# Splitting the contraction of narrow fp32 products into two row tiles, ordered through SyncE

## The chip, the core and the metric

The kernel runs on one core of a Trainium2 chip. The metric is the device time of one execution in microseconds. Two runs of the kernel before took 1523.30 and 1524.68 us, a median of 1523.99 us.

## What is computed

The reference, cut to what matters (B = 8, N = 4096, F = 256):

```python
HW = einsum('bnf,fo->bno', x, W)
A_norm = relu((adj + adj.T) * 0.5)
D = sum(A_norm, axis=1)
d = where(D > 0, D ** -0.5, 0)
L_norm = eye(N) - d[:, None] * A_norm * d[None, :]
out = relu(einsum('nm,bmo->bno', L_norm, HW))
return layernorm(x + out, axis=-1)
```

`adj` is sparse, and denser towards its first rows and columns.

## The kernel before

The first half of the kernel (to about 590 us) symmetrises `adj` in 512x512 blocks and writes it to the DRAM array `a_dram`, forms the scaled products `g = d * x W` (2048 columns: 8 batches of 256) and writes them to `g_dram`, and multiplies the first block of 128 output rows ("lead").

The last stage, which the change touches, computes the other 31 blocks of 128 output rows. They are taken in units `u` of two blocks, 2u+1 and 2u+2 (the last unit has one), in the order `SEQ`. Every row j of `g` gets a pattern of four bits for a unit: which of the four 64 row halves of the unit's two blocks have a nonzero among the 64 entries that meet it. Rows of one pattern ("kind") are listed, 128 to a list. For each list, `gather` (L797) issues two indirect DMAs on GpSimd: `ga` (L814), the 128 rows of `a_dram` that serve as the weights, and `g` (L827), the 128 rows of 2048 columns that stream through. A ring of 12 `g` tiles lets the gathers run ahead of the products.

`steps_of(u)` orders a unit's lists into steps. A step of kind 0, 3 or 12 has products of all 128 output rows of a block ("full"). A step of kinds 1+2, 4+8, 6, 9 or 5+10 has products of 64 output rows; most such steps have two that use different halves of TensorE's columns, some have four (two blocks), a few have one. At L1032 the products of a step are issued for c = 0 to 3, the four PSUM banks of 512 columns of each block:

```python
for c in range(G // S):
    for (b, rows, at, gt), new_rows in zip(work, fresh):
        ...
            nc.tensor.matmul(
                py[2 * u + 1 + b][c][rows, :],
                lhsT=at[:, off + rows.start : off + rows.stop],
                rhs=gt[:, c * S : (c + 1) * S],
```

What else belongs to a unit stands in the program's order around the products, written out by hand: `queue(engine)` ties an instruction behind the last one traced on that engine, and `after(n, fn)` defers work until n products later.

- When a block's last product is issued, `finish` lets ScalarE evict its four banks (`evict`, L683). A little later VectorE adds the residual (L693), takes the statistics (L702 and after) and an inverse root, and, three products later in program order, normalises (L726). Right behind it stands the store of the block on SyncE's queue, `nc.sync.dma_start(out...)` (L734).
- The first block of a unit ends in its steps of kinds 5+10 or before; the second ends with the unit's last step, 4+8 or 4.
- After the first block, TensorE runs the small products of the list building for later units (`lists`: L226 to L356), which VectorE reads and works on (`place`, `place_rest`, `index`). At the start of a unit `prepare` puts more list work on VectorE (`spread`, L335 to L351; `patterns`, L199 to L216).

In this stage SyncE does nothing but the 31 stores of whole blocks, and the four of the last block.

Of the kernel before, what the change touches and what calls it, by code (L numbers as in the profile page):

```python
# [59 lines left out]
def kernel(  # L60
# [25 lines left out]
    nc = tc.nc  # L86
    B, N, F = x.shape
    FO = w.shape[1]
    P = 128
    S = 512  # L90
# [4 lines left out]
    G = B * FO  # L95
# [2 lines left out]
    QU = 4  # L98
    HOLD = 10
    RING = 12  # L100
    EPS = 1e-5
    NK = len(KINDS)
    tiles = [sum(caps) for caps in CAPS]
# [71 lines left out]
    def blocks(u):  # L175

        return min(2, NB - 1 - 2 * u)
# [497 lines left out]
    def residual(i, engine):  # L675
        xr = blocks_pool.tile([P, B, F], F32, tag="adj", name=f"xr_{i}")
        engine.dma_start(xr, x[:, i * P : (i + 1) * P, :].rearrange("b p f -> p b f"))
        return xr
# [12 lines left out]
    def moments(i, y, z, stat):  # L691

        nc.vector.tensor_add(z, z, y)  # L693
        return statistics(i, z, stat)

    def statistics(i, z, stat, tag=""):
# [6 lines left out]
        for b in range(n):  # L703
            nc.vector.bn_aggr(mv[:, b, :], stats[:, b, :])
        nc.vector.tensor_scalar(rstd, mv[:, :, 1], EPS, None, ALU.add)
        return mv, rstd
# [32 lines left out]
    def targets(u, kind):  # L739

        if kind == 0:
            kind = 15 if blocks(u) == 2 else 3
        out = []
        for b in range(2):
            h = kind >> 2 * b & 3
            if h:
                out.append((b, {1: slice(0, Q), 2: slice(Q, P), 3: slice(0, P)}[h]))
        return out
# [19 lines left out]
    with (  # L768
        tc.tile_pool(name="ypool", bufs=2) as ypool,
        tc.tile_pool(name="rows", bufs=RING + 2) as apool,  # L770
        ExitStack() as gath,
    ):
        ring = [
            gath.enter_context(tc.tile_pool(name=f"gath_{k}", bufs=1)).tile([P, G], F32, name=f"g{k}")
            for k in range(RING)
        ]
# [9 lines left out]
            "pe": mybir.EngineType.PE,  # L786
            "act": mybir.EngineType.Activation,
            "dve": mybir.EngineType.DVE,
            "pool": mybir.EngineType.Pool,
        }  # L790

        def queue(engine):

            traced = reversed(nc.cur_bb.bb.instructions)
            return tc.issue_after(next(i for i in traced if i.engine == engines[engine]))

        def gather(n):  # L797

            if n >= len(order):
                return  # L800
            u, kind, t = order[n]
            both = len(targets(u, kind)) == 2
            at = apool.tile([P, 2 * P], F32, tag="a", name=f"ga_{u}_{t % tmax}")
            if t < 0:
                if not hub_loads:
                    with queue("pool"):
                        hub_loads.append(nc.gpsimd.dma_start(hub, g_dram[:P, :]))
                with queue("pool"):
                    nc.gpsimd.dma_start(at, a_dram[:P, (2 * u + 1) * P : (2 * u + 3) * P])
                got[u, t] = (at, hub)  # L810
                return
            gi, ai = plan[u]
            with queue("pool"):
                nc.gpsimd.indirect_dma_start(  # L814
                    out=at if both else at[:, :P],
                    out_offset=None,
                    in_=a_pairs if both else a_rows,
                    in_offset=bass.IndirectOffsetOnAxis(ap=ai[:, t : t + 1], axis=0),
                    element_offset=P if both else 0,
                )  # L820


            n = len(ring_tiles)
            gt = ring[n % RING]
            ring_tiles.append(gt)
            with queue("pool"):
                nc.gpsimd.indirect_dma_start(  # L827
                    out=gt,
                    out_offset=None,
                    in_=g_dram,  # L830
                    in_offset=bass.IndirectOffsetOnAxis(ap=gi[:, t : t + 1], axis=0),
                    bounds_check=N if n < RING else N - 1,
                    oob_is_err=False,
                )
            got[u, t] = (at, gt)
# [4 lines left out]
        def after(n, fn, *args):  # L840
            later.append((n, fn, args))
# [8 lines left out]
        u = SEQ[0]  # L850
        xr = {i: residual(i, nc.sync) for i in (0, *range(2 * u + 1, 2 * u + 1 + blocks(u)))}
        for n in range(RING):
            gather(n)
        n = RING
        py = {0: lead}
        left = {}
# [50 lines left out]
        def finish(i):  # L907

            if i == NB - 1:
                finish_last(i)  # L910
                return
            with queue("act"):
                y = evict(i, py.pop(i), ypool)

            def rest():
                z = xr.pop(i)
                with queue("dve"):
                    mv, var = moments(i, y, z, stat)
                with queue("dve"):
                    rstd = inverse_root(i, var, stat)  # L920

                def end():
                    in_turn(normalise, i, z, mv, rstd)

                after(3, end)

            after(1, rest)
# [59 lines left out]
        def in_turn(fn, *args):  # L987

            with queue("dve"):
                fn(*args)  # L990

        finish(0)
        side = None
        for q, (u, step) in enumerate(steps):
            new = q == 0 or steps[q - 1][0] != u
            last = q + 1 == len(steps) or steps[q + 1][0] != u
            if new:
                after(6, prepare, u)
                if q > 0:
                    after(10 if u != SEQ[-1] else 4, residuals, range(2 * u + 1, 2 * u + 1 + blocks(u)))  # L1000
                left = {}
                for v, st in steps[q:]:
                    if v == u:
                        for k, t in st:
                            for b, _ in targets(u, k):
                                left[b] = left.get(b, 0) + 1
                begun = set()
                for b in range(blocks(u)):
                    py[2 * u + 1 + b] = []
            work = [(b, rows, *got[u, t]) for m in range(2) for k, t in step for b, rows in targets(u, k)[m : m + 1]]  # L1010
            if work[0][1] == side != slice(0, P):
                work.reverse()
            side = work[-1][1]
            for b in sorted({wk[0] for wk in work}):
                if not py[2 * u + 1 + b]:
                    py[2 * u + 1 + b] = [
                        psum.tile([P, S], F32, tag=f"b{b}", name=f"py_{u}_{b}_{c}") for c in range(G // S)
                    ]
            fresh = []
            for b, rows, at, gt in work:  # L1020
                hs = {(b, h) for h in range(2) if rows.start <= h * Q < rows.stop}
                assert not hs & begun or hs <= begun
                fresh.append(not hs & begun)
                begun |= hs
                left[b] -= 1
            for c in range(G // S):
                for (b, rows, at, gt), new_rows in zip(work, fresh):
                    both = any(len(targets(u, k)) == 2 for k, t in step)
                    off = b * P if both else 0

                    with queue("pe"):
                        nc.tensor.matmul(  # L1032
                            py[2 * u + 1 + b][c][rows, :],
                            lhsT=at[:, off + rows.start : off + rows.stop],
                            rhs=gt[:, c * S : (c + 1) * S],
                            start=new_rows,
                            stop=left[b] == 0,
                            skip_group_check=True,
                        )
            for k, t in step:  # L1040
                gather(n)
                n += 1
            run_later(sum(1 + (rows == slice(0, P)) for _, rows, _, _ in work))
            for b in {wk[0] for wk in work}:
                if left[b] == 0:
                    finish(2 * u + 1 + b)
                    if b == 0:
                        after(2, lists, u)
# [9 lines left out]
    with tc.If(short > 0):  # L1058
        with (
# [4 lines left out]
            for i in range(NB):  # L1064
# [4 lines left out]
                py = [psum.tile([P, S], F32, tag="b0", name=f"pz_{i}_{c}") for c in range(G // S)]  # L1069
                for m in range(NB):  # L1070
                    gt = full.tile([P, G], F32, tag="g", name=f"gf_{i}_{m}", bufs=4)
                    nc.sync.dma_start(gt, g_dram[m * P : (m + 1) * P, :])
                    for c in range(G // S):
                        nc.tensor.matmul(
                            py[c],
                            lhsT=lt[:, m, :],
                            rhs=gt[:, c * S : (c + 1) * S],
                            start=(m == 0),
                            stop=(m == NB - 1),
# [33 lines left out]
```

## Time and profile before

| what | value |
| --- | --- |
| median of 2 runs | 1523.99 us |
| profiled execution, its span | 1527.5 us |
| last stage, first to last product of L1032 | 594.9 to 1513.8 us |
| mean granted TensorE clock | 0.981 |
| DMA, mean over the span | 370 GB/s |
| gathers of `g` (L827) / of `ga` (L814) on GpSimd | 268, mean 1101 ns / 268, mean 1090 ns |
| evictions (L683) | 120, mean 687 ns |
| residual adds (L693) | 31, mean 2294 ns |
| normalisations (L726) | 248 (eight per block), mean 409 ns |

How to read it: the profile is of one execution, and its span is the time from the first to the last instruction; the page's shares are of that span. A group's line has the line of the kernel, engine, operation, what is written and read, how often, busy time and mean length of one, and the idle time of the engine ahead of it with what ended it. Lengths of matmuls overlap, so a group's busy time is less than count times length. "128*64" is a matmul of 128 contracting rows and 64 columns of weights. Page slices and windows show the granted clock as PEclk.

### The profile page before, as it was taken

The page shows a single profiled execution, that of the slowest core. Times are in us where ns is not written, and L with a number is a line of the kernel's source. Part 1 is how long each engine was busy: PE and PEld are TensorE (multiplying, and loading weights), DVE is VectorE, ACT ScalarE, POOL GpSimd, SP SyncE. Part 2 cuts the span into 40 slices and gives each one's busy share as a digit, 9 for nine tenths or more (in the row PEclk, how much of TensorE's full clock was granted, in tenths as well). Part 3 has the DMA queues.
Part 4 walks back from the last instruction along what each step waited for, and adds up shares of the span by engine and source line. Part 5 has one row for each costly group of instructions (what it writes and reads, how often), then busy time and mean ns, then how long its engine had stood idle before and what let it go on. Part 6 is the DMA issues. An engine that isn't in the chain of part 4 may idle for free.

```text
span 1527.5 us, 19332 instructions
## 1 busy us (share of the span) xinstructions
PE 1441.2 (94%) x6440; PEld 763.6 (50%) x6440; DVE 983.6 (64%) x3015; ACT 369.0 (24%) x462; POOL 682.0 (45%) x1051
## 2 busy tenths in 40 slices
PE   5999999989989989999999999999999999999995
PEld 5778777767767754433343343333433433333331
DVE  4676578888646463055568769569137688898534
ACT  3655554535434450010100100100010010001111
POOL 3002010010303316666667666666556676656653
PEclk9999999989999999999999999999999999999998
DMA  9999999999879898999999999999979999999995
GB/s 340 365 366 401 393 379 365 359 369 354 344 248 367 332 390 354 401 395 418 361 393 372 402 409 365 393 403 389 384 278 406 346 394 403 405 393 366 379 405 195
DMA packets 216714, 564.50 MB, mean 370 GB/s; under 512 B 16550, under 2 KB 104918, under 8 KB 180134
## 3 DMA queue, kind: packets, MB, share of 16 engines
q0 software_dynamic: 54224, 304.94, 50.4%
q1 hardware_dynamic: 93472, 126.89, 23.8%
q10 hardware_dynamic: 68912, 131.37, 22.7%
q8 instruction: 54, 0.88, 0.2%
q14 instruction: 52, 0.43, 0.1%
HBM read 443.61 MB, written 136.34 MB: 380 GB/s over the span
## 4 chain that ended last, share of the span: by engine, by line
PE 68%; DMA 14%; DVE 9%; issue 5%; POOL 2%; ACT 2%; ACTq 0%; DVEq 0%; POOLq 0%
PE py L1032 49%; PE pg L532 8%; DMA g<-g_dram,gi 6%; PE lead L490 5%; DMA a_dram<-sym 5%; DVE sym L427 3%; PE xtr L521 2%; PE tr L423 2%; DVE part L432 2%; DMA xin<-in_x_dram 2%; DMA ga<-a_dram,ai 1%; ACT sym L431 1%; PE lists L356 1%; ACT xt L522 1%; POOL g L827 0%
## 5 line engine op out<-in xcount | busy, mean ns | idle before, releaser
L1032 PE MATMUL py<-g,ga 128*64 128x512 f32 (+1 forms) x2872 | 813.0, 600 | 18.4 <-DMA g<-g_dram,gi 8.0
L1032 PEld LDWEIGHTS py<-g,ga 128*64 128x64 f32 (+1 forms) x2872 | 293.1, 151 | 525.1 <-issue 493.1
L827 POOL DMA_INDIRECT g<-g_dram,gi x268 | 294.9, 1101 | 219.1 <-PE py L1032 79.1
L814 POOL DMA_INDIRECT ga<-a_dram,ai x268 | 292.0, 1090 | 109.5 <-issue 76.8
L683 ACT ACTIVATE y<-py,minus_r 128x512 f32<-128x512 f32 x120 | 79.9, 687 | 812.3 <-PE py L1032 659.8
L693 DVE TENSOR_TENSOR xr<-xr,y 128x2048 f32<-128x2048 f32 x31 | 71.1, 2294 | 269.1 <-ACT y L683 267.2
L532 PE MATMUL pg<-w_sb,xt 128*128 128x256 f32 x1024 | 232.0, 385 | 5.2 <-ACT xt L522 5.2
L427 DVE TENSOR_TENSOR sym<-tr,adj 128x512 f32<-128x512 f32 x256 | 162.7, 683 | 96.9 <-PE tr L423 80.2
L532 PEld LDWEIGHTS pg<-w_sb,xt 128*128 128x128 f32 x1024 | 195.6, 194 | 33.4 <-ACT xt L522 5.6
L432 DVE TENSOR_REDUCE part<-sym 128x32 f32<-128x2048 f32 x64 | 145.5, 2279 | 62.0 <-ACT sym L431 62.0
L423 PE MATMUL tr<-ident,adj 128*128 128x128 f32 x1024 | 138.4, 285 | 30.6 <-DVE sym L427 19.2
L431 ACT ACTIVATE sym<-sym 128x2048 f32<-128x2048 f32 x64 | 122.6, 1916 | 129.9 <-DVE sym L427 117.5
L452 POOL TENSOR_TENSOR r<-e,neg_half 128x4 f32<-128x4 f32 x8 | 8.3, 1039 | 317.9 <-DVE e L451 236.5
L423 PEld LDWEIGHTS tr<-ident,adj 128*128 128x128 f32 x1024 | 118.6, 146 | 60.4 <-DVE sym L427 32.1
L521 PE MATMUL xtr<-ident,xin 128*128 128x128 f32 x512 | 72.4, 288 | 18.0 <-DVE sym L427 16.5
L702 DVE BATCH_NORM_STATS2 stats<-xr 128x6 f32<-128x256 f32 x256 | 87.0, 413 | 1.1
L726 DVE TENSOR_SCALAR xr<-xr,mv,root 128x256 f32<-128x256 f32 x248 | 83.6, 409 | 0.1
L490 PE MATMUL lead<-gt,strip 128*128 128x512 f32 x176 | 83.0, 598 | 0.0
L522 ACT COPY xt<-xtr 128x512 f32<-128x512 f32 x128 | 68.1, 591 | 46.7 <-PE xtr L521 46.0
L542 ACT ACTIVATE gt<-pg,r 128x512 f32<-128x512 f32 x88 | 60.6, 688 | 74.8 <-PE pg L532 72.3
L1032 PE MATMUL py<-g_hub,ga 128*128 128x512 f32 x176 | 77.3, 592 | 0.0
L521 PEld LDWEIGHTS xtr<-ident,xin 128*128 128x128 f32 x512 | 59.0, 146 | 34.9 <-DVE sym L427 26.4
(142 smaller groups left out, 825.8 us busy)
## 6 DMA issues: line engine op xcount, KB each, us to landing
adj<-in_adj_dram SPq DMA_DIRECT2D x64, 1024.0 KB
a_dram<-sym ACTq DMA_DIRECT2D x64, 1024.0 KB
out_dram<-xr SPq DMA_DIRECT2D x31, 1024.0 KB
xr<-in_x_dram ACTq DMA_DIRECT2D x29, 1024.0 KB
xin<-in_x_dram SPq DMA_DIRECT2D x44, 512.0 KB
g_dram<-gt ACTq DMA_DIRECT2D x22, 1024.0 KB
xin<-in_x_dram POOLq DMA_DIRECT2D x20, 512.0 KB
g_dram<-held ACTq DMA_DIRECT2D x10, 1024.0 KB
```

The costliest lines, as they stand in the source:

```text
L423: ins = nc.tensor.transpose(pt[:, c * P : (c + 1) * P], tji[:, c, a * P : (a + 1) * P], ident)
L427: nc.vector.tensor_add(sym[:, a, :], pt, tij[:, a, :])
L431: nc.scalar.activation(sym, sym, AF.Relu, scale=0.5)
L432: nc.vector.tensor_reduce(part[:, i * A : (i + 1) * A, j * S // Q : (j + 1) * S // Q], sym.rearrange("p a (c q) -> p a c q", q=Q), AX.X, A ...
L490: nc.tensor.matmul(lead[c], lhsT=strip, rhs=g[:, c * S : (c + 1) * S], start=not done, stop=len(done) == NB - 1, skip_group_check=True,)
L521: nc.tensor.transpose(pt[:, k, c, :], xin[b // H][:, b % H + k, c * P : (c + 1) * P], ident)
L532: ins = nc.tensor.matmul(pg[:, k * FO : (k + 1) * FO], lhsT=xt[:, b + k, c, :], rhs=w_sb[:, c, :], start=(c == 0), stop=(c == FC - 1),)
L702: nc.vector.bn_stats(stats[:, b, :], z[:, b, :])
L726: nc.vector.tensor_scalar(z[:, b, :], z[:, b, :], mv[:, b, 0:1], rstd[:, b : b + 1], ALU.subtract, ALU.mult,)
L814: nc.gpsimd.indirect_dma_start(out=at if both else at[:, :P], out_offset=None, in_=a_pairs if both else a_rows, in_offset=bass.IndirectOff ...
L827: nc.gpsimd.indirect_dma_start(out=gt, out_offset=None, in_=g_dram, in_offset=bass.IndirectOffsetOnAxis(ap=gi[:, t : t + 1], axis=0), boun ...
L1032: nc.tensor.matmul(py[2 * u + 1 + b][c][rows, :], lhsT=at[:, off + rows.start : off + rows.stop], rhs=gt[:, c * S : (c + 1) * S], start=ne ...
```

## The change

A step whose products are all of 64 columns is split along the contracting rows (`KP = 2`): row tile 0 takes the partitions 0 to 63 of `ga` and `g`, row tile 1 the partitions 64 to 127. In group c, row tile 0 works on bank c and row tile 1 on bank (c + 2) % 4, so the two never write one bank in the same group. Full steps are as before.

From group c to c + 2 a bank passes from one row tile to the other. This order is kept through SyncE: after each group an empty instruction on SyncE (a "tick") waits for the group's last product, and the first product of the group after the next waits for that tick. The ticks are queued behind what was last traced on SyncE. In the program as built the tick is an event on SyncE's sequencer.

```diff
+    KP = 2
...
-            "pool": mybir.EngineType.Pool,
+            "pool": mybir.EngineType.Pool, "sp": mybir.EngineType.SP,
...
+        ticks = []
+
+        def follow(after_, before_):
+            tc.add_manual_dep(
+                after_.ins, before_.ins.name,
+                mybir.DependencyInfo(mybir.DependencyClass.Sync, mybir.DependencyReason.DATA),
+                reason="one bank, two row tiles",
+            )
...
+            few = all(rows.stop - rows.start < P for _, rows, _, _ in work)
+            nk = KP if few else 1
             for c in range(G // S):
-                for (b, rows, at, gt), new_rows in zip(work, fresh):
...
+                first_of_step = True
+                for kp in range(nk):
+                    cc = (c + kp * (G // S) // nk) % (G // S)
+                    ps = slice(kp * P // nk, (kp + 1) * P // nk)
+                    for (b, rows, at, gt), new_rows in zip(work, fresh):
...
+                            ins = nc.tensor.matmul(
+                                py[2 * u + 1 + b][cc][rows, :],
+                                lhsT=at[ps, off + rows.start : off + rows.stop],
+                                rhs=gt[ps, cc * S : (cc + 1) * S],
+                                start=new_rows and c < (G // S) // nk,
+                                stop=left[b] == 0 and c >= (nk - 1) * (G // S) // nk,
+                                skip_group_check=True,
+                            )
+                        if nk > 1:
+                            if first_of_step and len(ticks) > 1:
+                                follow(ins, ticks[-2])
+                            first_of_step = False
+                if nk > 1:
+                    with queue("sp"):
+                        ticks.append(nc.sync.nop())
+                    follow(ticks[-1], ins)
```

More of the change, by code (lines that the diff above doesn't have):

```diff
@@ L1025 @@
                 left[b] -= 1
+            few = all(rows.stop - rows.start < P for _, rows, _, _ in work)
+            nk = KP if few else 1
             for c in range(G // S):
-                for (b, rows, at, gt), new_rows in zip(work, fresh):
[L1028 to L1039, printed above, removed]
+                first_of_step = True
[3 more added lines that the diff above has]
+                    for (b, rows, at, gt), new_rows in zip(work, fresh):
+                        both = any(len(targets(u, k)) == 2 for k, t in step)
+                        off = b * P if both else 0
+                        with queue("pe"):
+                            ins = nc.tensor.matmul(
[14 more added lines that the diff above has]
+                    follow(ticks[-1], ins)
             for k, t in step:
```

## The prediction

> **What bounds the kernel now.** I read the page first, for the engine that carries the end:
>
> ```profile
> PE 1441.2 (94%) x6440; PEld 763.6 (50%) x6440; DVE 983.6 (64%) x3015; ACT 369.0 (24%) x462; POOL 682.0 (45%) x1051
> PE 68%; DMA 14%; DVE 9%; issue 5%; POOL 2%; ACT 2%; ACTq 0%; DVEq 0%; POOLq 0%
> ```
>
> TensorE is busy 94% of the span, and 68% of the chain that ended last is its own. The change touches only the last stage (594.9 us to the end), so I then asked for the groups with shapes kept apart:
>
> ```profile
> L1032 PE MATMUL py<-g,ga 128*64 128x512 f32 x2152 | 494.7, 601 | 14.9 <-DMA g<-g_dram,gi 8.0 <-issue 3.8 <-DVE pos_k L188 2.2
> L1032 PE MATMUL py<-g,ga 128*128 128x512 f32 x720 | 322.0, 597 | 3.5 <-issue 3.0
> ```
>
> The program has 1076 products of 64 columns and the trace 2152 records: an fp32 product is two passes. The timeline of TensorE shows their pace: in a full-width step a pass starts every 0.429 us, in a step with two 64 column products on different column halves two passes start within 7 ns every 0.429 us. So the halves already overlap: a bank's worth costs 0.858 us, whether one full product or two half-width ones. There are 121 steps of 64 column products: 100 with two products, 16 with four, 5 with one; 100 x 3.43 + 16 x 6.86 + 5 x 3.43 = 470 us, nearly their 494.7 busy.
>
> TensorE in turn feeds VectorE, and VectorE releases SyncE's stores. One unit, blocks 17 and 18, on VectorE's timeline:
>
> ```profile
> 1187.10 2.29 DVE L693 TENSOR_TENSOR xr<-xr,y 128x2048 f32<-128x2048 f32 x1 [7.49 <-ACT y L683]
> ...
> 1199.92 2.67 DVE L726 TENSOR_SCALAR xr<-xr,mv,root 128x256 f32<-128x256 f32 x8
> ...
> 1219.89 2.29 DVE L693 TENSOR_TENSOR xr<-xr,y 128x2048 f32<-128x2048 f32 x1
> ...
> 1235.80 2.87 DVE L726 TENSOR_SCALAR xr<-xr,mv,root 128x256 f32<-128x256 f32 x8
> ```
>
> The first column is the start, the second the length. VectorE waits for the unit's first block (7.49 us), then works nearly without a gap until the second is normalised. The two stores are issued at 1202.62 and 1238.69, within 0.03 us of those ends. SyncE's waits and the source view of the store say the same:
>
> ```profile
> SPq L734 <- DVE xr L726: 517.8, 17, 62.5
> L734 SPq DMA_DIRECT2D out_dram<-xr x31: 372/372/388, 614.6 to 1500.3; - x31
> ```
>
> SyncE stands waiting before each of 31 stores. Today nobody waits for SyncE.
>
> [...] after idling 2.37 us it ran 3.41 us at half clock:
>
> ```profile
> 933.47 8.04 PE L1032 MATMUL py<-g,ga 128*64 128x512 f32 x20 [2.37 <-DMA g<-g_dram,gi]
> 933.40:936.80 3.40, 3.33 (x8) 1.00 (x10) 3.13 (x10) 0.00 (x0) 1.99 (x2) 0.50 1.02 382
> 936.80:940.20 3.40, 3.40 (x12) 1.23 (x9) 3.37 (x6) 0.00 (x0) 2.45 (x2) 1.00 1.01 385
> ```
>
> Eight passes instead of 16 in 3.4 us: 3.41 / 2 = 1.7 us lost per such wait.
>
> **The change, part by part.**
>
> *The split.* 1076 products become 2152 of half the contracting rows. Per bank's worth, two tiles of 128x64 become four of 64x64; each still streams 512 columns in two passes. The two-product step already filled the array, so I take 0: the same 0.858 us. Bounds: if row tiles don't overlap, +470 us; if passes on 64 rows took half the time, -235 us. Neither is excluded by a row[...]. Weight loads double from 2152 to 4304 records, hidden: 137 ns each, side by side, in the 0.429 us of the pass before. Changes of tile shape stay as many as now (0.05 to 0.1 us at each, in the gaps between steps).
>
> *The ticks, as a handshake.* After each of 484 groups (one c of a step) SyncE waits for the group's last product; the next group but one waits for that tick. With groups of 0.858 us: the last pass starts 0.429 into its group and ends 0.592 later, at 1.02; the waiting group is due at 1.72 and wants its weights 0.14 earlier, so 0.55 us of cover. The round trip: TensorE to another engine 0.05 (ACT's eviction at 1231.13 against a pass that ends at 1231.08), SyncE's own event about 0.07 (its row of events at the end)[...]. [...] Each 0.1 us over the cover would cost 484 x 0.1 = 48 us. Groups of four products have twice the room.
>
> *The ticks, as a place in SyncE's queue.* The built program's order on SyncE: 4 ticks, a store, 29 ticks, a store, 19, a store, and so on; VectorE's and POOL's orders are unchanged, ACT's residual loads move ahead by two evictions (in its idle time, 812.3 us before L683: nothing). A store waits for VectorE's normalisation of its block, and every tick behind it waits too, hence TensorE two groups later, hence everything behind that matmul, the next block's products above all. So for each store: how late is it against the group that now needs it?
>
> First block of a unit (A): VectorE's lag from the block's last product to the store is 15.0 us when VectorE isn't behind (14.9 to 17.5 in twelve units). The order puts the needing group a constant 10.76 us of TensorE time after that product (block 17: 1186.33 to 1197.09). Issue 0.372, the tick and a cold restart add 0.55. Stall 15.0 + 0.55 - 10.76 = 4.8 us. Nine units have this: 43.2. The others by the same sum: block 9 3.0 (12.58 us away), 15 5.5, 23 6.6, 25 3.4, 27 3.8, 29 3.6 (the last three lag 10.9 to 12.4): 25.9. Block 0's store at 614.57 against a group at 607.29: 7.8.
>
> Second block (B): VectorE's work from store A to store B is fixed, 28 to 37 us up to block 24. TensorE, released at A, needs B's tick after its own time between the two groups. B stalls only where that is shorter: block 16, 30.0 against 14.1: 15.9; block 2, 33.5 against 28.7: 4.7; 18, 36.1 against 27.0: 9.1; 20, 32.8 against 28.1: 4.7; 22, 29.9 against 27.0: 3.0. Together 37.4. In the other units 0 (block 6: 36.9 against 39.8).
>
> So 7.8 + 43.2 + 25.9 + 37.4 = 114.3 us. Each of these 21 waits idles TensorE 3 us or more, so 1.7 us at half clock follows: 35.7, less 5 x 1.7 = 8.5 where an A's loss only shortens the B wait behind it: +27.2.
>
> *What the stalls give back.* The source view of L1032 has 15.6 us of waits for ga, 14.6 for g and 6.4 for VectorE's pos_k, 36.6 together, several soon after a store's group (5.2 us in the step at 930, 5.9 in the one at 982). While TensorE stands, gathers land and VectorE catches up. I take half, -18; ends 0 and -36.6.
>
> Sum: 114.3 + 27.2 - 18 = +123 us. The profiled execution spans 1527.5, the median of the runs is 1523.99; the sum is on the span, 1650, so 1647 for a median.
>
> **Rivals.**
>
> 1. *Row tiles don't overlap in fp32.* Then the 470 us double. The distance of 10.76 us holds two pair steps (6.9), so it becomes 17.6, over 15.55: A stalls go. 1524 + 470 = 1994. For it: nothing here runs row tiles. Against: column halves overlap perfectly.
> 2. *The handshake is late as well.* At 0.2 us over the cover in some 430 groups, +86 us: about 1733. For it: SyncE's answer to TensorE is unseen. Against: the hops that are seen take under 0.1 us.
> 3. *Not slower: ticks aren't held by the stores.* Place: SyncE's queue before each store. If VectorE's normalisation came within 10.76 - 0.55 = 10.2 us of the last product, or ticks passed a waiting store, the price is 0, and 1524 to 1530 follows. Against: the lag is 11 to 17 us at A, and SyncE's events after a store run only once it is issued.
> 4. *A faster pass.* -235 us, but needing groups then come 3.4 us sooner: (4.8 + 3.4 + 1.7) x 15 of A, about 149, plus some 60 of B, where VectorE's 51 us from block A's last product to store B then bounds most units: about 1500.
>
> **How the numbers follow.** Likeliest, 66%: 1647, own range 1610 to 1690 (give-back 0 to -36.6, lag by a microsecond). Rival 2 14%, rival 1 10%, rival 3 6%, rival 4 4%. The range 1595 to 1770 holds the likeliest and rival 2 and leaves the rest out, 2 in 10. 2% is about what a measurement of this kernel can tell from no change. Slower 0.90 (likeliest, 1, 2), same 0.08 (3 and half of 4), faster 0.02.
>
> **What would show it.** Right: passes of 64 columns still 0.429 us apart, four starts together; TensorE idle about 5 us once or twice per unit, ended by SyncE; about 20 more stretches of half clock; VectorE busy as before (some 984 us); SyncE's stores again at VectorE's ends. Step by step: the pace tests the split, the time from tick to the next group the handshake, the idle before the group after a store the queue. Wrong: pairs 0.858 us apart (rival 1), small idle times in every group (2), no idle after stores (3).

## The result, and the profile after

The changed kernel took 1639.47 us (median of two runs, 1638.16 to 1640.78) against 1523.99 us: 1.0761 times as long, with a 95% interval of 1.073 to 1.0793. The prediction said 1647 us. Ratios in this document are taken over the fast executions alone, so they can differ a little from the quotient of two medians. The profiled execution spans 1639.1 us; the last stage runs from 596.5 to 1626.1 us, 110 us longer than before.

The engines' line and the chain of the page after:

```profile
PE 1468.2 (90%) x8592; PEld 795.2 (49%) x8592; DVE 980.0 (60%) x3015; ACT 365.8 (22%) x462; POOL 707.7 (43%) x1051
PE 41%; DVE 25%; DMA 13%; issue 12%; POOL 7%; ACT 2%; SPq 0%; ACTq 0%; POOLq 0%; DVEq 0%
```

TensorE is still the busiest, but its share of the chain fell from 68% to 41%, and VectorE's rose from 9% to 25%: the chain now runs through VectorE's normalisation and a store to TensorE. The groups of products, with shapes kept apart:

```profile
L1048 PE MATMUL py<-g,ga 64*64 64x512 f32 x4304 | 521.0, 624 | 103.8 <-SPq L1062 103.8
L1048 PE MATMUL py<-g,ga 128*128 128x512 f32 x720 | 320.4, 598 | 0.0
```

The full products are as they were. The split ones doubled in number, hardly in busy time (521.0 for 494.7), and carry 103.8 us of idle time, all ended by L1062, the tick. Waits for gathers and for VectorE's `pos_k`, 36.6 us of TensorE's queue before, are no longer in the list. VectorE in the unit of blocks 17 and 18, and SyncE's waits before the stores:

```profile
1253.63 2.29 DVE L694 TENSOR_TENSOR xr<-xr,y 128x2048 f32<-128x2048 f32 x1 [19.18 <-ACT y L684]
...
1265.26 2.83 DVE L727 TENSOR_SCALAR xr<-xr,mv,root 128x256 f32<-128x256 f32 x8
...
1279.35 2.29 DVE L694 TENSOR_TENSOR xr<-xr,y 128x2048 f32<-128x2048 f32 x1
...
1295.20 2.67 DVE L727 TENSOR_SCALAR xr<-xr,mv,root 128x256 f32<-128x256 f32 x8
```

```profile
SPq L735 <- DVE xr L727: 260.6, 19, 21.1
```

The first store is issued at 1268.12, within 0.1 us of the end of its normalisation (1265.26 + 2.83), the second at 1297.89. Between these two VectorE needs 29.8 us; before it needed 36.1 in this unit. TensorE around the first store:

```profile
1257.05 6.24 PE L1048 MATMUL py<-g,ga 64*64 64x512 f32 x56
1268.60 17.13 PE L1048 MATMUL py<-g,ga 64*64 64x512 f32 x88 [5.31 <-SPq L1062]
```

```profile
1263.10:1266.50 3.40, 0.19 (x4) 0.00 (x0) 3.30 (x9) 1.27 (x2) 2.49 (x4) 0.94 0.93 359
1266.50:1269.90 3.40, 1.30 (x8) 0.55 (x12) 3.16 (x17) 0.00 (x0) 0.49 (x1) 0.50 1.01 388
```

TensorE stops at 1263.29 and goes on at 1268.60, 0.48 us after the store was issued (0.55 in the prediction, of which 0.372 is the measured issue and the rest its author's estimate). In the windows (TensorE's busy time is the first number after the length, the granted clock the third from the end) it restarts at half clock (0.50).

### The profile page after: what moved, and what is told of

It reads as the page before. It is cut to its first block, busy times and chain, and to the rows that moved or that the text cites. A ratio compares the mean times of both kernels' runs of the same rounds, so it can differ in the third digit from the quotient of the medians.

```text
span 1639.1 us, 24158 instructions
## 1 busy us (share of the span) xinstructions
PE 1468.2 (90%) x8592; PEld 795.2 (49%) x8592; DVE 980.0 (60%) x3015; ACT 365.8 (22%) x462; POOL 707.7 (43%) x1051
## 4 chain that ended last, share of the span: by engine, by line
PE 41%; DVE 25%; DMA 13%; issue 12%; POOL 7%; ACT 2%; SPq 0%; ACTq 0%; POOLq 0%; DVEq 0%
PE py L1048 24%; PE pg L533 8%; DMA g<-g_dram,gi 5%; PE lead L491 4%; DMA a_dram<-sym 4%; DVE xr L727 4%; POOL ga L815 3%; POOL g L828 3%; DVE sym L428 3%; PE xtr L522 2%; PE tr L424 2%; DVE part L433 2%; DVE stats L703 2%; DVE hot L336 2%; DVE xr L694 2%
## 5 line engine op out<-in xcount | busy, mean ns | idle before, releaser
L1048 PE MATMUL py<-g,ga 64*64 64x512 f32 (+1 forms) x5024 | 837.6, 621 | 103.8 <-SPq L1062 103.8
L1048 PEld LDWEIGHTS py<-g,ga 64*64 64x64 f32 (+1 forms) x5024 | 321.6, 147 | 606.8 <-issue 388.3
L828 POOL DMA_INDIRECT g<-g_dram,gi x268 | 302.1, 1127 | 307.1 <-PE py L1048 252.8
L815 POOL DMA_INDIRECT ga<-a_dram,ai x268 | 310.7, 1159 | 90.5 <-issue 82.6
L684 ACT ACTIVATE y<-py,minus_r 128x512 f32<-128x512 f32 x120 | 76.1, 685 | 930.1 <-PE py L1048 912.4
L533 PEld LDWEIGHTS pg<-w_sb,xt 128*128 128x128 f32 x1024 | 196.0, 194 | 33.5 <-ACT xt L523 5.6
```

The lines of the kernel that those rows point to most:

```text
L533: ins = nc.tensor.matmul(pg[:, k * FO : (k + 1) * FO], lhsT=xt[:, b + k, c, :], rhs=w_sb[:, c, :], start=(c == 0), stop=(c == FC - 1),)
L815: nc.gpsimd.indirect_dma_start(out=at if both else at[:, :P], out_offset=None, in_=a_pairs if both else a_rows, in_offset=bass.IndirectOff ...
L828: nc.gpsimd.indirect_dma_start(out=gt, out_offset=None, in_=g_dram, in_offset=bass.IndirectOffsetOnAxis(ap=gi[:, t : t + 1], axis=0), boun ...
L1048: ins = nc.tensor.matmul(py[2 * u + 1 + b][cc][rows, :], lhsT=at[ps, off + rows.start : off + rows.stop], rhs=gt[ps, cc * S : (cc + 1) * S ...
```

## The experiments

All times are medians of four or more runs, each beside runs of the kernel before on the same chip (1522.21 and 1523.83 us on one chip, 1533.67 and 1533.44 on two others); ratios are to these. Where a kernel moves a store, it moves nothing else on any engine.

### The ticks alone

```diff
-            nk = KP if few else 1
+            nk = 1
...
-                        if nk > 1:
+                        if few:
...
-                if nk > 1:
+                if few:
```

> The products stay whole as in the kernel before (128 listed columns, one row tile); only SyncE's ticks stay, 484 of them at the same places in the queues, and TensorE still waits for the tick two groups back. Theory (the loss is the ticks' place behind the waiting stores): as slow as the changed kernel, 1639 us, within 1625 to 1650; TensorE idle some 104 us in about 22 gaps that SyncE's tick ends, 5 us each for most. Rival (row tiles of 64 rows cost time on TensorE, in passes or weight loads): 1524 to 1535, as before, since no row tile is left. Rival (both share it): in between, about 1580.

Measured: 1601.04 us, 1.0527 (1.0494 to 1.056), less than the 1625 to 1650 expected. Without any row tile most of the loss is there, and TensorE's waits are again the tick's:

```profile
PE py L1048 <- SPq L1062: 73.9, 20, 18.9
```

So most of the loss needs no row tile; ticks in this place are enough. But 38 us of it are missing. The order of the built program shows that this kernel has the stores of first blocks three ticks later: after 36, 76, 108 ticks instead of 33, 73, 105 (with one product in place of two the store is placed at the end of its step). That is 3 x 0.858 = 2.57 us more room. The gaps at the nine usual first blocks are 1.9 to 2.4 us instead of 4.9 to 5.3. Another 0.5 us of the difference is the split's own. ScalarE's evictions of block 3, in this kernel and then in the changed one:

```profile
667.22 0.69 ACT L684 ACTIVATE y<-py,minus_r 128x512 f32<-128x512 f32 x1 [70.52 <-PE py L1048]
668.94 0.69 ACT L684 ACTIVATE y<-py,minus_r 128x512 f32<-128x512 f32 x1 [1.03 <-PE py L1048]
670.65 0.69 ACT L684 ACTIVATE y<-py,minus_r 128x512 f32<-128x512 f32 x1 [1.03 <-PE py L1048]
672.37 0.69 ACT L684 ACTIVATE y<-py,minus_r 128x512 f32<-128x512 f32 x1 [1.03 <-PE py L1048]
```

```profile
671.19 1.27 ACT L684 ACTIVATE y<-py,minus_r 128x512 f32<-128x512 f32 x2 [73.93 <-PE py L1048]
672.91 1.26 ACT L684 ACTIVATE y<-py,minus_r 128x512 f32<-128x512 f32 x2 [0.45 <-PE py L1048]
```

Whole products finish one bank per group, and ScalarE takes each as it comes. Split ones finish the four banks in the last two groups, two at a time, so the last eviction ends 1.25 us after the block's last product (674.17 against 672.92) instead of 0.74 (673.06 against 672.32). VectorE's lag at the nine usual first blocks becomes 15.4 to 15.8 us instead of 14.9 to 15.3.

In this kernel TensorE's idle time in the stage is 78.6 us against 103.8 and its loss at half clock (half of the busy time in such stretches) 18.3 us against 34.6. Together that is 41.5 us less; the stage is 42.1 us nearer to the time at full pace. Within the idle time the nine usual first blocks have 27 us less and the other six 25 us less, and the second blocks have 28 us more (44 against 16): much of what is not waited for at the first store is waited for at the second.

### All stores late

```diff
                     in_turn(normalise, i, z, mv, rstd)
+                    after(14, send)
+
+                def send():
+                    with queue("sp"):
+                        store(i, z)
```

(`store` is the DMA of L735, taken out of `normalise`.)

> The split and all ticks stay; only the stores of blocks 0 to 30 are put 14 half-width products (about 24 us of TensorE) later into SyncE's queue, behind the ticks that they held up. Nothing else changes its order on any engine. Theory (place behind the stores): 1524 to 1535 us, no gap on TensorE that a tick ends beyond one of 2 us, half clock back to about 6 us; VectorE's work from the first to the second store of a unit back to 28 to 37 us, as in the kernel before, since TensorE no longer gives it rests. Rival (the split costs time): stays over 1600. Rival (the round trip of a tick is late by itself): 484 small gaps, each 0.1 us of them 48 us, so 1570 or more.

Measured: 1534.03 us, 1.0075 (1.005 to 1.0101); in a second set of runs 1532.02 us, 1.0063 (1.0042 to 1.0083). Ticks, handshake and row tiles are all there, and about 105 of the 115 us are gone:

```profile
PE py L1055 <- SPq L1069: 4.9, 1, 4.9
PE py L1055 <- DMA g<-g_dram,gi: 4.5, 3, 1.9
PE py L1055 <- DVE pos_k L189: 3.4, 1, 3.4
```

The old waits for gathers and `pos_k` are back. One tick is still late by 4.9 us. It stands behind one more instruction of SyncE's in this stage, which the description of the kernel before does not list: the load of the flag at L1088, which waits for VectorE too. One expectation failed: VectorE's work from first to second normalisation did not return to 28 to 37 us. It is 29.8 to 30.9 us in the units up to block 22, with no stalls to rest in. So the rests are not what made it shorter.

### Only first blocks, only second blocks

```diff
-                    after(14, send)
+                    if i % 2 or i == 0:
+                        after(14, send)
+                    else:
+                        in_turn(store, i, z)
```

The second kernel has the two branches the other way round.

> As the changed kernel, but only the stores of a unit's first block (and block 0) are put 14 half-width products later in SyncE's queue; those of second blocks stay. Theory (stalls at second blocks are hidden behind those at first blocks, and come out when these are gone): 29 to 48 us of stalls at second blocks by a sum over the places (about 6 at block 2, 7 to 14 at block 18, 6 to 9 at blocks 20, 22), 4 to 5 of them with 1.7 us of half clock, some give-back of 8: 1550 to 1580 us, likeliest 1565. Rival (the gaps that the changed kernel shows are each worth their own length, first and second blocks apart): only block 16's and small ones are left at most, so 1525 to 1540.

> As the changed kernel, but only the stores of a unit's second block are put 14 half-width products later; those of first blocks stay where they are. Theory: the 16 stalls at first blocks stay, about 80 us, with 27 us of half clock, less 17 that the old waits give back: 1614 us (1600 to 1625). VectorE's work between the two stores stays at 30 us, as the rests at first blocks are still there. Rival (second blocks carry a good part of the loss, as the prediction had it with 37 us and their half clock): 1590 or less.

Measured: with the first blocks' stores late 1618.81 us, 1.0647 (1.0623 to 1.067); with the second blocks' late 1621.76 us, 1.0659 (1.0633 to 1.0684). TensorE's waits for the ticks in the one and in the other:

```profile
PE py L1058 <- SPq L1072: 80.4, 12, 21.0
```

```profile
PE py L1058 <- SPq L1072: 83.0, 16, 7.6
```

The second is as the theory had it, 83.0 us in 16 gaps of the same lengths as in the changed kernel. The first was much slower than the 1565 us expected, though it goes the way of the theory and against the rival. The expectation overlooked that block 16's store stands ahead of block 15's when that one is late, so its whole wait of 21 us stays:

```profile
1049.51 8.48 PE L1058 MATMUL py<-g,ga 128*128 128x512 f32 x31
1078.94 6.58 PE L1058 MATMUL py<-g,ga 64*64 64x512 f32 x20 [20.96 <-SPq L1072]
```

Nor did it count that in units whose old waits disappear TensorE reaches the tick that much sooner (5.9 us at block 12, 5.1 at block 14, where 0 was expected). So with one kind of store in the way the loss is 97 or 100 us, with both 115, with neither 10. Neither kind alone can be credited with its own gaps: a wait at the first store lets VectorE come nearer to the second.

### Three ticks later, and a handshake without cover

These ran on a second chip. The first has `send()` in place of `after(14, send)` for all blocks; the second that for first blocks, with `after(14, send)` kept for second blocks; the third has all stores late and

```diff
-                            if first_of_step and len(ticks) > 1:
-                                follow(ins, ticks[-2])
+                            if first_of_step and len(ticks) > 0:
+                                follow(ins, ticks[-1])
```

the fourth has the whole products of the first experiment with all stores late.

> The changed kernel with each store tied behind the last tick, which puts the stores of first blocks 3 ticks (2.57 us of TensorE) later into SyncE's queue, and the second blocks' nowhere. That is the queue order that the run with whole products and ticks had (1601 us, 1.0527 of before), so the two differ by the split alone. Theory (the split costs TensorE nothing, but a block's banks are now complete two by two in the last groups, so VectorE's lag is 0.5 us longer, 15.5 against 15.0): 1601 + 15 x 0.5 + up to 10 us of half clock from gaps of 2.5 instead of 2.0 us = 1609 to 1620. Rival (the split itself makes up the 38 us between the run with whole products and the changed kernel): 1635 to 1640. Rival (it costs nothing at all): 1601.

> Stores of second blocks 14 half-width products later, those of first blocks 3 ticks later. Theory: the gaps at first blocks shrink by 2.57 us each, from 5.0 to 5.3 down to 2.4 to 2.7, and second blocks have none: idle 45 us in 15 gaps, half clock 15 to 25 us, give-back of 15, 12 as the run with all stores late had: 1575 us (1565 to 1590). [...] Rival (half clock follows every wait, 1.7 us and more each): 1590 to 1600.

> All stores late (that alone gave 1.0075 of before), and every group waits for the tick of the group just before it, not the one before that, so the round trip over SyncE has no cover. Theory: a group takes its last product's end (1.02 us after its start) plus the round trip of 0.2 to 0.4 us with the weights, 1.25 to 1.45 us against 0.86; for 420 groups of two products and 64 of four: 190 to 285 us more, 1725 to 1820 us. From it follows the round trip itself, which must be under the 0.55 us of cover that the prediction counted. Rival (the round trip is longer than that cover and already showed): over 1880. Rival (the wait is nearly free, under 0.1 us): under 1680.

> Whole products, ticks kept, all stores 14 half-width products later: the run with all stores late, without the split. Theory (what that run had over the kernel before, 0.5 to 1.0%, comes from the stores that end later and not from the split): ratio to before 1.003 to 1.010, 1527 to 1537 us. Rival (the split costs these 12 us): ratio 0.998 to 1.002.

Measured: 1674.28 us (1.0934, 1.0882 to 1.0986), 1652.86 us (1.0804, 1.0753 to 1.0854), 1808.95 us (1.1786, 1.1729 to 1.1842) and 1646.6 us (1.0684, 1.0615 to 1.0754). Three of the four are far from what was expected. The last has no row tile and no store in the way, and should have cost nothing. Its waits name a new thing. SyncE's waits, and TensorE around two of them:

```profile
SPq L1069 <- PE py L1055: 767.6, 367, 51.6
...
SPq L1069 <- remote: 183.2, 37, 10.0
```

```profile
674.93 1.94 PE L1055 MATMUL py<-g,ga 128*64 128x512 f32 x8
680.14 13.28 PE L1055 MATMUL py<-g,ga 128*64 128x512 f32 x40 [3.27 <-SPq L1069]
```

```profile
679.11 0.17 DVE L722 SCALAR_TENSOR_TENSOR root<-half,root 128x8 f32<-128x8 f32 x1
680.00 0.18 DVE L369 COPY low<-lists 128x19 f32<-128x19 f32 x1 [0.73 <-remote]
```

"remote" means that the profile has no instruction that ended just before the wait did. TensorE's products end at 676.87, the ticks that wait for them run at 680.08 and 680.15, and VectorE's L369, which waits for list products that ended at 675.0, starts at 680.00. Three waiters for TensorE's signals are released within 0.15 us of each other, 3 to 5 us late. About 70 of the 484 ticks come more than 0.6 us after their product; in the ticks-alone run on the first chip the median is 0.04 us and the late ones are those behind stores. The runs of late signals also lack part of the semaphore records (1177 of 1264 of TensorE's; on the first chip none of these is missing).

The third run still shows the bare round trip where signals are on time: a group of two products takes 1.21 us instead of 0.858. The tick comes 0.06 us after the product's end and TensorE starts 0.06 us after the tick, so the hops are 0.12 us, well under the 0.55 us of cover. The 1809 us lie in the expected span, but late signals are part of them.

### The same again

To see whether the lateness belongs to a kernel or to the occasion, four of the kernels ran again, in two sets.

> The run with all stores late again (1.0075 of before at first), beside the one with whole products, ticks and late stores, which came out at 1.0684 on another occasion, with TensorE's signals to SyncE 2 to 6 us late in about 70 of 484 ticks. Theory (in some executions signals between engines are late in bursts, whatever the products; it depends on the chip or the occasion, not on the kernel): both kernels within 2% of each other here, either both near 1.01 or both near 1.07. Rival (whole products with ticks are slow by themselves, split ones are not): 1.0075 here and 1.07 for the other.

> Whole products, ticks, all stores late, again, on the same chip as the split kernel with late stores. Theory (the delay of signals belongs to the occasion; the split costs nothing): as that kernel, within 1%; if the signals come on time, 1.003 to 1.010 of before. Rival (whole products with ticks are slow by themselves): 1.05 to 1.08 while the other stays at 1.0075.

Measured, both on the first chip: 1532.02 us, 1.0063 (1.0042 to 1.0083), and 1524.73 us, 1.0008 (0.9994 to 1.0023). The kernel that took 1.0684 takes no measurable time more here, with

```profile
SPq L1069 <- PE py L1055: 874.1, 480, 51.6
```

and no "remote". So the lateness is not this kernel's. And 484 ticks with nothing in their way cost nothing that can be measured, and neither do late stores, for which 1.003 to 1.010 was expected. The pair differs by 7.3 us, which is what is left for the split with late stores. TensorE's idle time in the stage is the same in both (14.1 and 14.2 us), but in the split kernel it lies in longer gaps (4.9 us at the flag's load, which stands four ticks earlier there, and 3.6 at `pos_k`), and 5.5 us of half clock follow, where the other has none.

> The changed kernel with the stores of first blocks 3 ticks later, again, where the first time signals between engines were late (1.0934 of before). With signals on time: the queue order of the run with whole products and ticks (1.0527 of before), so the ratio of the two is the split: 0.5% directly, as the pair with late stores showed (1.0063 against 1.0008), and 0.5 us of VectorE's lag at each first block with some half clock for it: 1.060 to 1.070 of before, 1613 to 1630 us. Rival (the split costs nothing under a held queue): 1.053. With signals late again: 1.09.

> Stores of second blocks late, those of first blocks 3 ticks later, again, where the first time signals between engines were late (1.0804 of before). With signals on time: gaps of 2.4 to 2.7 us at first blocks instead of 5.0 to 5.3, none at second blocks: idle 45 us, half clock 15 to 25, 1.030 to 1.045 of before, 1575 us. With signals late again: 1.08.

Measured, on a third chip: 1680.96 us, 1.0997 (1.0918 to 1.1077), and 1668.92 us, 1.0923 (1.0856 to 1.0989), with 197.7 and 194.3 us of "remote" waits of SyncE: signals were late again. What these two were to tell, the split under a held queue against the ticks-alone run and the worth of shorter gaps, was not measured with signals on time. It rests on the account of idle time and half clock under the first experiment.

## Why the prediction was right

1. *The split, 0.* Right on TensorE. Pair steps take 3.43 to 3.48 us and full ones 6.87 as before, and four tiles of 64x64 start within 22 ns of each other every 0.429 us, the pace of two of 128x64. Not foreseen: the banks complete in pairs, which is 0.5 us of VectorE's lag at ten of the fifteen first blocks. In all the split is worth 7 us with the stores out of the way. Rival 1 (1994 us) and rival 4 (a faster pass) fall with the same pace. Row tiles without the handshake were not tried, as two of them would then write one bank without an order; no run shows what that would do.
2. *The handshake, 0.* Right where signals are on time: 0.12 us for the two hops, under the 0.55 us of cover that the prediction counted, and 1.0008 for ticks alone with late stores. That the way back from SyncE would be short enough was its author's estimate; the trace of before does not show it. On a second chip a loss of rival 2's kind is real, though by bursts of late signals and not by a little at every group: with them that same kernel took 6.8% more than the kernel before. The changed kernel itself was not run there. Its profile has signals on time.
3. *The place behind the stores, 114.3.* Right, with the run of late stores as the proof (1534.03 us; rival 3 falls: in the trace after, the tick behind the store issued at 1268.12 runs at 1268.54, 5.2 us after TensorE stopped). By the same classes the trace after has: block 0 7.6 us (7.8 predicted); the nine usual first blocks 46.1 (43.2), 0.3 each more since the lag grew; the other six 28.8 (25.9); second blocks 16.0 (37.4); block 30 5.3 (0). That is 103.8.
4. *The term that was off* is the second blocks. The step took VectorE's work from store to store, "28 to 37 us", from the trace of before as fixed, and read VectorE there as working "nearly without a gap". In the unit of blocks 17 and 18 VectorE is busy for 29.0 of the 36.1 us before, and for 28.2 of 29.8 us after. Much of the rest before, 5.7 us, is idle time between small dependent instructions, most of which wait for VectorE's own instruction just before; after, there is none of it:

```profile
1208.11 0.16 DVE L263 TENSOR_TENSOR free<-upto,off 128x2 f32<-128x2 f32 x1 [0.54 <-DVE upto L262]
...
1210.24 0.16 DVE L262 TENSOR_TENSOR upto<-upto,total 128x2 f32<-128x2 f32 x1 [1.60 <-remote]
```

   That trace also lacks records of TensorE's semaphore (877 of 928). These are the marks of late signals, which the prediction read as the length of the work. One program run on two chips shows the same: whole products with late stores need 32.0 to 37.4 us from store to store up to block 22 where signals are late, and 30.0 to 30.8 us where they are on time. In all kernels on the first chip it is 29.7 to 31.1 us there, stalled or not, and in the changed kernel's trace 29.8 to 30.8. With 29.8 in the place of 33.5, 36.1 and 32.8, and everything else kept, the waits at second blocks come to 24.4 us instead of 37.4, and the 114.3 to 101.3. The 8.5 us that the prediction takes off in its half clock term come off these same waits: 24.4 - 8.5 = 15.9, against 16.0 measured.
5. *Half clock, +27.2.* Measured 34.6 us after against 6.5 before, +28.1. That these agree so closely is luck. Counted as in item 4 the prediction has 35.7 us, and no term takes off the 6.5 us of before. It has one stretch of 3.41 us at half clock, 1.7 us lost, for each of 21 waits, and expects about 20 more stretches. The trace after has 17 stretches, 13 more than before, and 11 of the 17 last 6.83 us or more.
6. *The give-back, -18.* It was half of 36.6 us of waits, with no reason given for the half. These include waits of weight loads during which products ran; TensorE's own idle time in the stage was 18.4 us before (14.9 + 3.5 in the groups' lines). All of that is gone, and stalls at ticks have its place. So the number agrees, but not by the prediction's way to it. Not foreseen: a store further on takes some of it, as block 30's with 5.3 us, though that this is the reason there is argued only.

The sum then reads 103.8 - 18.4 + 28.1 = 113.5 us, against the 110 us by which the stage became longer and the 115 of the medians. The prediction's +123 was 21 us too much at second blocks and 11 too little at the rest. The mechanism was right; that the total came within 8 us owes something to errors of opposite sign.

## What to carry to other kernels

An empty instruction that keeps an order cost here what stood ahead of it in its engine's queue (115 us behind the stores, and with whole products and late stores no time that can be measured, 1.0008): list every waiting instruction of that queue, and compare when it is released with when the first needed signal behind it is due. Where a queue has waits at several places, don't add their prices: an earlier stall gives the producer of the next one time (with the ticks alone 52 us less at first stores came with 28 us more at second ones), so removing one kind of wait alone recovered little (here 16 or 19 us of 115). Moving the store behind the signals, with nothing else touched, recovered nearly all (105 of 115).

A length that is read between two events holds every late signal between them (here 36.1 us in the trace before against 29.8 in the trace after). Before taking it as work, look for gaps between short dependent instructions and for waits that the profile can't name.

## What was not expected of the hardware

The price of a gap did not follow from its length alone. In the traces before and after, all stretches of half clock (12 and 26 in the whole execution) start on one grid of 3.413 us per trace, to within 6 ns; "window" here means the time from one line of that grid to the next. The changed kernel's gap of 3.50 us at block 9, cut by the grid (columns as above):

```profile
893.96:897.37 3.41, 1.71 (x16) 0.31 (x8) 3.31 (x9) 0.00 (x0) 2.71 (x3) 1.00 0.85 294
897.37:900.79 3.42, 1.62 (x16) 0.67 (x20) 3.18 (x18) 0.00 (x0) 2.16 (x3) 1.00 0.94 353
900.79:904.20 3.41, 3.41 (x36) 1.44 (x32) 3.10 (x27) 2.42 (x4) 1.60 (x2) 1.00 1.01 310
```

and a gap of 2.06 us at the same block with the ticks alone:

```profile
879.87:883.28 3.41, 1.34 (x8) 0.48 (x8) 3.17 (x18) 0.82 (x2) 1.55 (x2) 1.00 1.03 316
883.28:886.69 3.41, 3.41 (x10) 0.98 (x8) 3.10 (x27) 1.24 (x2) 2.26 (x3) 0.50 0.88 278
```

The longer gap, 1.7 and 1.8 us in two windows, is followed by no half clock (1.00 in all three); the shorter one, whole in one window, is followed by a clock of 0.50 in the next. Over the 568 windows of the last stage in the traces before and after, a full-clock window idle for 1.77 us or less was never followed by half clock, and one idle for 2.17 us or more always was; of the two in between, the one idle for 1.81 us was and the one idle for 1.95 us was not. Half clock ended only after windows idle for 0.60 us or less and went on after every one idle for 0.76 us or more; 10 of the 17 stretches after last two windows (6.83 us). So the price of a gap here depended on where the grid cut it.

Signals came late in bursts (about 70 of 484 ticks by more than 0.6 us). One program shows it in the run on one chip (three waits released 3 to 5 us late in the stretch above) and not in the run on another. On a third chip the two kernels that ran had waits of the same kind; these two were never run with signals on time, so there the chip and the kernel can't be told apart. The kernel before carries the marks too, in its profile, though its median of 1523.99 us is that of the runs on the first chip; TensorE, which waits for no tick there, has only 18.4 us of idle time in the stage. All of these traces lack records of signals, so whether the recording itself is part of the cause stays open; no run here is without it.
